# Attention and ternary FFN on one core: SP's DMA queue put into the program's order from the second unit on

## The chip, the core and the metric

One core of one Trainium2 chip runs the whole kernel in one launch. The metric is the device time of one execution in microseconds (us). The kernel before takes 1697.4 us (median of three executions, 1696.96 to 1698.08).

Engines go by the profile's names: PE (matmuls; PEld are its weight loads), DVE (vector), ACT (scalar), POOL (GpSimd) and SP. SP computes nothing here: it issues all DMAs, one after the other. When the next DMA in its program has to wait for data, everything behind that DMA waits too.

## The reference

x is 8 x 1024 x 256 in fp32. With LN a layernorm without weights:

```python
x = x + LN(attention(LN(x)) @ Wo)
x = x + LN(ffn(LN(x)))
# attention: q = h @ Wq (16 heads of 16), k, v = h @ Wk, h @ Wv (4 heads, each shared by 4 query heads);
#   rotary embedding on q and k; softmax(q k^T / sqrt(256)) v, no mask
# ffn: (h @ ternary(W).T) * alpha + bias, ternary(W) in {-1, 0, 1} by a threshold on mean |W|
```

## The kernel before

The 8192 rows are cut into 16 **units** of 512 queries; two units make one batch. A unit is worked through as four numbers i (i = 4u + j, j from 0 to 3; one head of each group for all 512 queries), each i in 8 **steps** (one tile of 128 keys), each step in four **quarter steps**. So a unit has 128 quarter steps. In one quarter step PE makes one matmul of scores for the exponentials (se, L676), one matmul of scores for the row maxima of a later i (sm, L603), and some matmuls of values (av, L712). ACT takes the exponentials (e, L692), DVE the maxima (mx, L628).

The softmax shift of an i goes into the score product itself: its maxima are joined (mc, L645), transposed on PE (pm, L651), copied by ACT (mh, L653), split by DVE (ml, L660) and written by two 8-KB DMAs (q_st<-ml, L667, function `shift_low`) into rows of the stacked queries q_st. The first se matmul of that i reads those rows, so it waits for the first of the two DMAs.

Beside this main loop run two chains that are cut into parts. Each part is put at a step of a unit by a table:

- **Project** (table P_PARTS) makes queries, keys and values of a unit three units ahead: layernorm, transposes (pt_xt), products (pkv, pq), rotary embedding on POOL. Keys go through DRAM twice: d_k<-kv_t (L434) and back as k_rot (L438, in `kv_and_dram`), then dk<-ks (L451, in `kt`, four DMAs) and back into the stacked keys k_st (L502, `stack_keys`, six DMAs). Queries go out as dq<-hlq (L493, `q_to_dram`, four DMAs). A unit ahead of their use they come back as q_st (L567, `stack_queries`: six DMAs of 256 KB and two fills, L146). I call these eight DMAs the **stack**.
- **Tail** (table T_PARTS) finishes the unit before. The sums av go to DRAM, one store for each i (d_av<-avsb, L733). `fetch` loads them as xn (L763, two DMAs) and their denominators as den (L768). `invert` takes the reciprocal on DVE, stores it (d_rec<-den, L775) and loads it spread over the rows (a<-d_rec, L780, two DMAs). `scale` multiplies xn by a on POOL (L786) and splits the result into a high and a low part, hl (L157, L162). `attn` multiplies hl by Wo on PE (pa, L302). Then follow layernorms, residual sums, the FFN (pt_ot, pf) and the store out_x<-a (L856, in `end`). A product pa reads hl of both halves c of the features. It makes the products of the high parts first and those of the low parts last.

What orders the work: the function `window` writes out the main loop, two to four quarter steps at a time, and puts due parts behind them. Inside `manual_schedule` the named engines keep the order in which the code issues; all others are ordered by a list scheduler at build time. For PE, DVE and ACT the order is written by hand in the whole loop. SP and POOL are ordered by the scheduler. Each DMA uses one of eight semaphores in turn, so it waits until the DMA eight places before it has landed.

Of the kernel before, what the change touches and what calls it, by code (L numbers as in the profile page):

```python
# [8 lines left out]
F32 = mybir.dt.float32  # L9
# [7 lines left out]
P = 128  # L17
# [3 lines left out]
HD = 16  # L21
UT = 4
UQ = UT * P
# [5 lines left out]
def kernel(  # L29
# [29 lines left out]
    nc = tc.nc  # L59
    B, S, D = x.shape  # L60
    DK = HKV * HD
# [7 lines left out]
    SPU = G * NK  # L69
# [5 lines left out]
    small = ctx.enter_context(tc.tile_pool(name="small", bufs=4))  # L75
    work = ctx.enter_context(tc.tile_pool(name="work", bufs=2))
    qkp = ctx.enter_context(tc.tile_pool(name="qkp", bufs=1))
# [29 lines left out]
    for src, lo, n in ((w_q, 0, D), (w_k, D, DK), (w_v, ROT, DK)):  # L107
        nc.sync.dma_start(
            out=wqkv[:, :, lo : lo + n], in_=src.rearrange("(c p) n -> p c n", p=P)
# [18 lines left out]
    nc.sync.dma_start(out=bias_bc, in_=bias.partition_broadcast(P))  # L128
    alpha_bc = const.tile([P, 1], F32, name="alpha_bc")
    nc.sync.dma_start(out=alpha_bc, in_=alpha.partition_broadcast(P))  # L130


    k_st, v_aug, q_st = [], [], []
# [30 lines left out]
    def split(eng, hi, lo, src, hi_eng=None):  # L164

        split_hi(hi_eng or eng, hi, src)
        split_lo(eng, lo, src, hi)
# [25 lines left out]
    ffn = {}  # L193
# [119 lines left out]
    def rotate(eng, x, cos, sin, t2):  # L313

        for dst, table in ((t2, sin), (x, cos)):
            eng.tensor_tensor(dst, x, table.unsqueeze(1).to_broadcast(list(x.shape)), ALU.mult)  # L316
        eng.tensor_tensor(x[:, 0], x[:, 0], t2[:, 1], ALU.subtract)
        eng.tensor_tensor(x[:, 1], x[:, 1], t2[:, 0], ALU.add)
# [5 lines left out]
    class Project:  # L324
# [103 lines left out]
        def kv_and_dram(self):  # L428

            u = self.u  # L430
            for p in range(2):
                self.kv(p)
            d_k = dram.tile([DK, UQ], F32, tag="d_k", name=f"d_k_{u}")
            nc.sync.dma_start(out=d_k, in_=self.kv_t[:DK])  # L434
            self.k_rot = qkp.tile([P, 2, P], F32, tag="k_rot", name=f"k_rot_{u}")
            src = d_k.rearrange("(m e) (g t) -> e g m t", e=2, t=P)
            for e in range(2):
                nc.sync.dma_start(out=self.k_rot[:, e, :], in_=src[e])  # L438

        def kt(self):  # L440
            rotate(
                self.eng, self.k_rot, cos_kt_sb[:, self.half], sin_kt_sb[:, self.half],
                work.tile([P, 2, P], F32, tag="t2k", name=f"t2k_{self.u}", bufs=1),
            )
            hl = qkp.tile([P, 2, 2, P], F32R, tag="k_parts", name=f"ks_{self.u}")
            split(self.eng, hl[:, 0], hl[:, 1], self.k_rot)
            dk = self.dk = dram.tile([2, DK, UQ], F32, tag="dk", name=f"dk_{self.u}")
            dst = dk.rearrange("l (m e) (g t) -> l e g m t", e=2, t=P)
            for l in range(2):
                for e in range(2):  # L450
                    nc.sync.dma_start(out=dst[l, e], in_=hl[:, l, e, :].bitcast(F32))  # L451
            self.stack_keys()

        def q_product(self, p):
            if self.q_rot is None:
# [31 lines left out]
        def q_to_dram(self):  # L487
            dq[self.u] = dram.tile([2, D, UQ], F32, tag="dq", name=f"dq_{self.u}")
            rows = dq[self.u].rearrange("l (b c i e) t -> l c b i (e t)", c=2, e=2, i=HD // 2)
            for l in range(2):  # L490
                for c in range(2):
                    src = self.hl["q"][64 * c : 64 * (c + 1), l].rearrange("p e t -> p (e t)")
                    nc.sync.dma_start(out=rows[l, c], in_=src.bitcast(F32))  # L493
# [176 lines left out]
    es, av_ps, av_sb, d_av = {}, {}, {}, {}  # L670
# [65 lines left out]
    class Tail:  # L736
# [21 lines left out]

        def fetch(self):

            for c in range(2):
                self.on[c] = self.new("xn", c)
                nc.sync.dma_start(  # L763
                    out=self.on[c].rearrange("p t d -> p (t d)"),
                    in_=d_av[self.u][8 * c : 8 * c + 8, 0:HD, :],
                )
            self.den = small.tile([P, UQ // 8], F32, tag="den", name=f"den_{self.u}", bufs=1)
            nc.sync.dma_start(  # L768
                out=self.den, in_=d_av[self.u][:, HD, :].rearrange("i (g t) -> i g t", g=8)
            )  # L770

        def invert(self):
            nc.vector.reciprocal(self.den, self.den)
            d_rec = dram.tile([2, 2 * HKV, UQ], F32, tag="d_rec", name=f"d_rec_{self.u}")
            nc.sync.dma_start(  # L775
                out=d_rec.rearrange("c i (g t) -> (c i g) t", g=8), in_=self.den
            )
            for c in range(2):
                self.a[c] = self.new("a", c)
                nc.sync.dma_start(  # L780
                    out=self.a[c].rearrange("p t d -> p (t d)"),
                    in_=d_rec[c].unsqueeze(1).to_broadcast([2 * HKV, HD, UQ]),
                )
# [66 lines left out]
        def end(self, p):  # L850
            u, f = self.u, self.a[p]
            ln_apply(self.eng(p), f, f, self.sc[p])
            self.eng(p).tensor_tensor(f, self.x1[p], f, ALU.add)
            b, half = divmod(u, UPB)
            tiles = out[b, half * UQ : (half + 1) * UQ, :].rearrange("(t p) d -> p t d", p=P)
            nc.sync.dma_start(out=tiles[:, self.tiles(p), :], in_=f)  # L856

    class LastTail(Tail):

# [76 lines left out]
    def at(step, f, *args):  # L936
        assert step >= -START
        todo.setdefault(step, []).append((f, args))
# [22 lines left out]
    def load(u):  # L961
# [3 lines left out]

    P_PARTS = (
        (26, "begin", 0), (33, "xw", 0), (37, "begin", 1), (43, "xw", 1), (49, "kv_and_dram"), (51, "q", 0), (52, "kt"), (53, "v"), (55, "q", 1),
        (57, "q_to_dram"),
    )
    L_PARTS = (  # L970
        (10, "n", 0), (13, "o", 0), (15, "attn", 0), (16, "stats_a", 0), (19, "stats_x", 0),
# [2 lines left out]
        (29, "attn", 2), (29, "x", 1), (30, "stats_a", 2), (30, "ffn", 1), (31, "stats_f", 1),  # L974
    )
    T_PARTS = (
        (1, "fetch"), (7, "invert"), (8, "scale", 0), (9, "scale", 1), (12, "attn", 0),
        (15, "attn", 1), (15, "stats_a", 0), (17, "stats_a", 1), (19, "stats_x", 0),
        (22, "xw", 0), (23, "stats_x", 1), (26, "ffn", 0), (27, "xw", 1), (31, "ffn", 1),
        (31, "stats_f", 0), (33, "stats_f", 1),  # L980
    )

    P_FIRST = (47, 51, 54, 57, 59, 60, 62, 61, 63, 64)
    T_LAST = (1, 3, 4, 5, 9, 10, 11, 14, 17, 19, 20, 22, 25, 27, 24, 28)

    warm = []

# [60 lines left out]
        for k, (_, *p) in zip(steps, P_PARTS):  # L1048
            at(start + k, part, projects, u, *p)
    for u in range(2, NU):  # L1050
        at(SPU * (u - 1) + 1, stack_queries, u)
    for u in range(NU - 1):
        start = SPU * (u + 1)
        at(start + 1, begin_tail, u)
        steps = [k for k, *_ in T_PARTS] if u < NU - 2 else T_LAST
        for k, (_, *p) in zip(steps, T_PARTS):
# [5 lines left out]
    def maxima_by(s):  # L1062

        return s + 4 * START + 2 * sum(s >= k for k in (28, 36, 52, 68, 84, 100))
# [13 lines left out]
    def window_size(s):  # L1078


        left = 4 * NK - s % (4 * NK)
        if s >= ends:
            return 4
        if s == 6:
            return 2
        size = min(2 if s >= REGULAR and any(banked(*p) for p in ready) else 3, left, ends - s)
        if left - size == 1:
            size += 1 if size == 2 else -1
        return size
# [23 lines left out]
    def take_low():  # L1113
        while split_later:
            shift_low(split_later.pop(0))
# [12 lines left out]
    def av_windows(lag):  # L1128

        while len(behind) > lag:  # L1130
            i, s, size = behind.pop(0)
            first = s % (4 * NK)
            av_piece(i, first * P, (first + size) * P)
            if first + size == 4 * NK:
                done.append(i)

    def window(s):


        late, size = s >= ends, window_size(s)  # L1140
        if done:
            av_out(done.pop())
        if late:
            for r2 in range(2):
                exp_two(s // 4, r2)
        else:
            end = min(maxima_by(s + size), 4 * NSTEP)
            for q in range(max(size, end - maxima[0])):
                if q < size:
                    exp_one(s + q)  # L1150
                if maxima[0] < end:
                    max_scores(maxima[0])
                    maxima[0] += 1
                if q == 0:
                    take_low()
            reduce_early(maxima[0])
        take_low()
        behind.append((s // (4 * NK), s, size))
        for n in range(s // 4, (s + size) // 4):
            collect(n)  # L1160
        do_parts(3 - size if REGULAR <= s < ends else 99)
        av_windows(1 if late else 2)
        return s + size

    E = mybir.EngineType
    due, picks = [], []
    with tc.manual_schedule(engines={E.PE, E.DVE, E.Activation, E.Pool}):
# [52 lines left out]
        s = 0  # L1220
        while s < 8:
            s = window(s)
    with tc.manual_schedule(engines={E.PE, E.DVE, E.Activation}):
        while s < 4 * NSTEP:
            s = window(s)
        av_windows(0)
        av_out(NU * G - 1)
        assert not (todo or due or ready or split_later)
# [70 lines left out]
```

## Time and profile before

| | |
|---|---|
| time, median of three executions | 1697.4 us |
| the profiled execution: its own time, its span | 1696.64 us, 1694.9 us |
| mean granted TensorE clock | 0.972 |
| busy: PE, DVE, ACT, POOL | 94%, 83%, 74%, 49% |
| DMA queue of SP | 115.60 MB, its packets 29.4% of 16 engines' span |
| chain that ended last | PE 59%, DVE 22%, DMA 9% |

How to read it. A unit takes 98.7 to 102.5 us in units 2 to 12 (from its first se matmul to the next unit's), so a stall of 1 us that comes once in each unit costs about 1% of the time. A row "X <- Y: total, times, longest" says how long X stood idle until Y ended. Rows of the timeline begin with the start in us from the beginning of the span, then the length; for SP the length is only the issuing, not the transfer. The granted clock is 1.00 or 0.50 at any moment; a mean between them says how much of the stretch ran at half speed.

### The profile page before, as it was taken

The numbers are of one execution on the slowest core, as the hardware profiler recorded it, in microseconds if no ns is written. First come the engines' busy times: TensorE is split into PE (matmuls) and PEld (weight loads), VectorE is DVE, ScalarE is ACT, GpSimd is POOL, SyncE is SP. The second block draws the span as 40 slices with busy tenths as digits, with TensorE's granted clock in tenths as the row PEclk, the third lists the DMA queues.
The fourth block names the chain that finished last, engine by engine and source line by source line (L and its number), as shares of the span: only waits on it lengthen the run. The fifth ranks groups of instructions, "written<-read, shape, count | busy, mean of one in ns | idle before, by whom it ended". The sixth has DMA issues, their size and how long they took to land.

```text
span 1694.9 us, 36717 instructions
## 1 busy us (share of the span) xinstructions
PE 1598.8 (94%) x14440; PEld 811.3 (48%) x14440; DVE 1398.7 (83%) x2054; ACT 1246.4 (74%) x2423; POOL 838.5 (49%) x1239
## 2 busy tenths in 40 slices
PE   7989899999999999999999999999999999999997
PEld 5544454444545444444444445444444544444444
DVE  7778788979798797978889798797978879998864
ACT  4657677778687786877778687686867768787875
POOL 5541456374554646455464645536455453333444
PEclk8999999999999999999999999999999999999999
DMA  4151514125151432515133151412415124141100
GB/s 134 51 98 37 122 43 95 54 73 98 48 98 57 81 72 65 113 42 100 49 86 80 54 115 45 94 55 71 88 46 100 36 76 74 33 85 33 41 14 26
DMA packets 86077, 117.95 MB, mean 70 GB/s; under 512 B 12088, under 2 KB 50808, under 8 KB 85752
## 3 DMA queue, kind: packets, MB, share of 16 engines
q1 hardware_dynamic: 85904, 115.60, 29.4%
q8 instruction: 114, 1.87, 0.5%
q14 instruction: 59, 0.48, 0.1%
HBM read 68.65 MB, written 45.88 MB: 68 GB/s over the span
## 4 chain that ended last, share of the span: by engine, by line
PE 59%; DVE 22%; DMA 9%; POOL 3%; issue 3%; SPq 2%; ACT 2%; POOLq 0%; ACTq 0%; DVEq 0%
PE av L712 21%; PE se L676 19%; DVE mx L628 18%; PE sm L603 8%; PE pa L302 3%; DMA q_st<-ml 2%; PE pq L302 2%; PE pf L302 2%; DMA dk<-ks 2%; DMA k_rot<-d_k 2%; PE pkv L302 1%; DVE bnst L237 1%; PE pt_ot L279 1%; DMA d_k<-kv_t 1%; ACT e L692 1%
## 5 line engine op out<-in xcount | busy, mean ns | idle before, releaser
L628 DVE TENSOR_REDUCE mx<-sm 128x2 f32<-128x1024 f32 (+1 forms) x1309 | 1205.2, 970 | 244.5 <-PE sm L603 191.3
L692 ACT ACTIVATE e<-se 128x512 f32<-128x512 f32 x1996 | 1053.2, 603 | 301.4 <-PE sm L603 256.6
L603 PE MATMUL sm<-k_st,q_st 64*128 64x512 f32 x2048 | 756.6, 453 | 16.6 <-DVE mx L628 7.7
L676 PE MATMUL se<-q_st,k_st 64*128 64x512 f32 x2048 | 721.7, 448 | 48.4 <-DMA q_st<-ml 42.7
L712 PE MATMUL av<-e,v_aug 128*32 128x256 f32 (+2 forms) x8560 | 612.1, 383 | 0.0
L676 PEld LDWEIGHTS se<-q_st,k_st 64*128 64x128 f32 x2048 | 330.0, 187 | 418.6 <-ACT e L692 240.2
L603 PEld LDWEIGHTS sm<-k_st,q_st 64*128 64x128 f32 x2048 | 329.1, 188 | 94.5 <-DVE mx L628 73.3
L712 PEld LDWEIGHTS av<-e,v_aug 128*32 128x32 f32 x8560 | 196.7, 109 | 233.6 <-issue 171.6
L241 POOL TENSOR_SCALAR lnsc<-mv 128x2 f32<-128x2 f32 (+1 forms) x134 | 25.8, 193 | 287.2 <-DVE mv L239 280.8
L786 POOL TENSOR_TENSOR xn<-xn,a 128x512 f32<-128x512 f32 x30 | 38.5, 1284 | 156.3 <-DMA a<-d_rec 153.9
L242 POOL TENSOR_TENSOR lnsc<-lnsc,mhalf 128x2 f32<-128x2 f32 (+1 forms) x134 | 92.5, 691 | 0.9
L846 POOL TENSOR_TENSOR a<-a,bias_bc 128x512 f32<-128x512 f32 x30 | 38.6, 1285 | 97.9 <-ACT a L845 97.9
L253 POOL TENSOR_SCALAR xn<-x,lnsc 128x256 f32<-128x256 f32 x116 | 65.1, 569 | 2.2
L157 POOL TENSOR_SCALAR ot<-ot 128x512 fp32r<-128x512 f32 x30 | 18.6, 621 | 83.9 <-ACT ot L283 63.7
L316 POOL TENSOR_TENSOR t<-q_rot,sin_q_sb 128x512 f32<-128x512 f32 x31 | 39.8, 1285 | 39.9 <-ACT q_rot L460 39.9
L157 POOL TENSOR_SCALAR xt<-xt 128x512 fp32r<-128x512 f32 x26 | 16.2, 622 | 65.3 <-ACT xt L283 65.3
L302 PE MATMUL pq<-xt,wqkvh 128*128 128x256 f32 x256 | 47.9, 313 | 0.4 <-ACT e L692 0.4
L302 PE MATMUL pa<-woh,hl 128*128 128x256 f32 x240 | 46.2, 294 | 1.1 <-ACT e L692 1.1
L237 DVE BATCH_NORM_STATS2 bnst<-x 128x6 f32<-128x256 f32 x124 | 45.9, 412 | 0.6 <-DMA x<-in_L_attn_x 0.6
L237 DVE BATCH_NORM_STATS2 bnst<-a 128x6 f32<-128x256 f32 x120 | 44.5, 413 | 0.0
L302 PEld LDWEIGHTS pq<-xt,wqkvh 128*128 128x128 f32 x256 | 38.3, 208 | 13.0 <-issue 11.6
L162 POOL TENSOR_TENSOR hlq<-q_rot,hlq 128x512 fp32r<-128x512 f32 x31 | 39.5, 1275 | 7.0 <-ACT hlq L159 4.5
(165 smaller groups left out, 1298.0 us busy)
## 6 DMA issues: line engine op xcount, KB each, us to landing
q_st<-dq SPq DMA_DIRECT2D x90, 256.0 KB
dq<-hlq SPq DMA_DIRECT2D x60, 256.0 KB
d_av<-avsb SPq DMA_DIRECT2D x60, 256.0 KB
x<-in_L_attn_x SPq DMA_DIRECT2D x15, 512.0 KB
xn<-d_av SPq DMA_DIRECT2D x30, 256.0 KB
a<-d_rec SPq DMA_DIRECT2D x30, 256.0 KB
xr<-in_L_attn_x SPq DMA_DIRECT2D x15, 512.0 KB
out_x<-a SPq DMA_DIRECT2D x30, 256.0 KB
```

Source lines behind the costliest of these rows:

```text
L162: eng.tensor_tensor(lo, src, hi.bitcast(F32), ALU.subtract)
L237: nc.vector.bn_stats(st[:, t, :], src[:, t, :])
L242: nc.gpsimd.tensor_tensor(sc[:, 1, :], sc[:, 1, :], mhalf[:, :n], ALU.pow)
L253: eng.tensor_scalar(dst[:, t, :], src[:, t, :], sc[:, 0, t : t + 1] if eng is nc.gpsimd else mv[:, t, 0:1], sc[:, 1, t : t + 1], ALU.add i ...
L302: nc.tensor.matmul(out, chunk(left[i], c), chunk(right[j], c), start=(k == 0), stop=(k == len(steps) - 1),)
L316: eng.tensor_tensor(dst, x, table.unsqueeze(1).to_broadcast(list(x.shape)), ALU.mult)
L603: scores = nc.tensor.matmul(sm[0][:, part, :], queries[rows], k_st[(u // UPB) % 3][rows, r2, ch * 512 : (ch + 1) * 512], start=True, stop= ...
L628: early[0] = nc.vector.tensor_reduce(mx[i][:, a, head_and_tile(i, r2, t), lo:n], sm[0][:, lo:n, :], AX.X, ALU.max).ins
L676: nc.tensor.matmul(sc if len(queries.shape) == 2 else sc.rearrange("p (j t) -> p j t", j=G), k_st[(i // G // UPB) % 3][rows, r2, kt * P : ...
L692: nc.scalar.activation(e, sc, AF.Exp, scale=1.0 / D**0.5)
L712: nc.tensor.matmul(av_ps[0][32 * r : 32 * r + 32, lo:hi], va[:, kt, r, :], es[i * NK + kt, r // 2, r % 2][:, lo:hi], start=(kt == 0 and lo ...
L846: eng.tensor_tensor(f, f, bias, ALU.add)
```

## The change

From quarter step 128 on (the second unit), SP too is ordered by hand. Transfers whose data come late are put into a list by `later(n, f)` and issued n windows further down. `fetch` loads the denominators ahead of the sums. `stack_queries` moves from step 1 to step 6 of its unit, `q_to_dram` from 57 to 62, and the early parts of the tail by one to three steps; DVE's and PE's parts move along with them. POOL stays with the scheduler.

```diff
+    def later(windows, f):
+        if running[0]:
+            postponed.append((window_number[0] + windows, f))
+        else:
+            f()
+    def queue_postponed(all_of_them=False):
+        for entry in list(postponed):
+            if all_of_them or entry[0] <= window_number[0]:
+                postponed.remove(entry)
+                entry[1]()
...
 # kv_and_dram
-            nc.sync.dma_start(out=d_k, in_=self.kv_t[:DK])
...
+            later(1, lambda: nc.sync.dma_start(out=d_k, in_=self.kv_t[:DK]))
+            later(3, fetch)          # fetch(): the two loads of k_rot
...
 # kt
+            later(4, store)          # store(): the four stores dk<-ks
+            later(7, self.stack_keys)
...
 # Tail.fetch: den<-d_av now ahead of the two xn<-d_av
 # Tail.invert
+            later(1, ...)            # d_rec<-den
+            later(3, lambda: self.load_factors(d_rec))   # the two loads a<-d_rec
 # Tail.end
-            nc.sync.dma_start(out=tiles[:, self.tiles(p), :], in_=f)
+            later(3, lambda: nc.sync.dma_start(out=tiles[:, self.tiles(p), :], in_=f))
...
-        (57, "q_to_dram"),
+        (62, "q_to_dram"),
...
     T_PARTS = (
-        (1, "fetch"), (7, "invert"), (8, "scale", 0), (9, "scale", 1), (12, "attn", 0),
-        (15, "attn", 1), (15, "stats_a", 0), (17, "stats_a", 1), (19, "stats_x", 0),
-        (22, "xw", 0), (23, "stats_x", 1), (26, "ffn", 0), (27, "xw", 1), (31, "ffn", 1),
+        (1, "fetch"), (7, "invert"), (10, "scale", 0), (11, "scale", 1), (14, "attn", 0),
+        (16, "attn", 1), (16, "stats_a", 0), (18, "stats_a", 1), (20, "stats_x", 0),
+        (23, "xw", 0), (24, "stats_x", 1), (27, "ffn", 0), (28, "xw", 1), (31, "ffn", 1),
...
-    T_LAST = (1, 3, 4, 5, 9, 10, 11, 14, 17, 19, 20, 22, 25, 27, 24, 28)
+    T_LAST = (1, 5, 8, 9, 11, 12, 13, 15, 17, 19, 20, 22, 25, 27, 24, 28)
...
-        at(SPU * (u - 1) + 1, stack_queries, u)
+        at(SPU * (u - 1) + 6, stack_queries, u)
...
 # window
+        window_number[0] += 1
+        running[0] = s >= 4 * SPU
...
+        queue_postponed()            # behind the window's se and sm, ahead of its parts
...
     with tc.manual_schedule(engines={E.PE, E.DVE, E.Activation}):
+        while s < 4 * SPU:
+            s = window(s)
+    with tc.manual_schedule(engines={E.PE, E.DVE, E.Activation, E.SP}):
         while s < 4 * NSTEP:
             s = window(s)
+        running[0] = False
+        queue_postponed(True)
```

In the built programs the middle of a unit on SP reads, before: dk x4, k_st x6, q_st<-ml (j = 3), xn_0, d_av, dq x4, q_st<-ml (j = 0), the stack, d_av, out_x, xn_1, den, out_x, q_st<-ml (j = 1), d_rec, a x2, d_av, q_st<-ml (j = 2), d_av, d_k, k_rot x2. After: d_av, out_x, xr, den, xn x2, out_x, q_st<-ml (j = 1), the stack, d_rec, d_av, a x2, q_st<-ml (j = 2), d_av, d_k, k_rot x2, x, q_st<-ml (j = 3), dk x4, d_av, k_st x6, q_st<-ml (j = 0), dq x4. (Here the j given is that of the i whose shift is written.)

More of the change, by code (lines that the diff above doesn't have):

```diff
@@ L130 @@
     nc.sync.dma_start(out=alpha_bc, in_=alpha.partition_broadcast(P))
+    postponed, window_number, running = [], [0], [False]
+    def later(windows, f):
[8 more added lines that the diff above has]
+                entry[1]()
     k_st, v_aug, q_st = [], [], []
@@ L433, in kv_and_dram, with fetch @@
             d_k = dram.tile([DK, UQ], F32, tag="d_k", name=f"d_k_{u}")
-            nc.sync.dma_start(out=d_k, in_=self.kv_t[:DK])
[L435 to L438, printed above, removed]
+            def fetch():
+                self.k_rot = qkp.tile([P, 2, P], F32, tag="k_rot", name=f"k_rot_{u}")
+                src = d_k.rearrange("(m e) (g t) -> e g m t", e=2, t=P)
+                for e in range(2):
+                    nc.sync.dma_start(out=self.k_rot[:, e, :], in_=src[e])
+            later(1, lambda: nc.sync.dma_start(out=d_k, in_=self.kv_t[:DK]))
+            later(3, fetch)
         def kt(self):
@@ L448, in kt, with store @@
             dst = dk.rearrange("l (m e) (g t) -> l e g m t", e=2, t=P)
[L449 to L452, printed above, removed]
+            def store():
+                for l in range(2):
+                    for e in range(2):
+                        nc.sync.dma_start(out=dst[l, e], in_=hl[:, l, e, :].bitcast(F32))
+            later(4, store)
+            later(7, self.stack_keys)
         def q_product(self, p):
@@ L489, in q_to_dram, with store_q @@
             rows = dq[self.u].rearrange("l (b c i e) t -> l c b i (e t)", c=2, e=2, i=HD // 2)
+            self.store_q(rows)
+        def store_q(self, rows):
             for l in range(2):
@@ L759, in fetch @@
         def fetch(self):
+            self.den = small.tile([P, UQ // 8], F32, tag="den", name=f"den_{self.u}", bufs=1)
+            nc.sync.dma_start(
+                out=self.den, in_=d_av[self.u][:, HD, :].rearrange("i (g t) -> i g t", g=8)
+            )
             for c in range(2):
@@ L766, in fetch @@
                 )
[L767 to L770, printed above, removed]
         def invert(self):
@@ L774, in invert, with load_factors @@
             d_rec = dram.tile([2, 2 * HKV, UQ], F32, tag="d_rec", name=f"d_rec_{self.u}")
-            nc.sync.dma_start(
+            later(1, lambda: nc.sync.dma_start(
                 out=d_rec.rearrange("c i (g t) -> (c i g) t", g=8), in_=self.den
-            )
+            ))
+            later(3, lambda: self.load_factors(d_rec))
+        def load_factors(self, d_rec):
             for c in range(2):
```

## Prediction

> **What bounds the kernel now.** I read the page's busy shares first, then PE's waits, SP's timeline, and busy time by stretch around the longest wait.
>
> ```profile
> PE 1598.8 (94%) x14440; PEld 811.3 (48%) x14440; DVE 1398.7 (83%) x2054; ACT 1246.4 (74%) x2423; POOL 838.5 (49%) x1239
> ```
>
> PE sets the pace; what can be gained is its idle and slow time. PE's waits have one large row:
>
> ```profile
> PE se L676 <- DMA q_st<-ml: 42.7, 16, 5.7
> ```
>
> The first score matmul of an i waits for its shift row. From the second unit on there are 13 such stalls: 5.77 us in unit 1 (i = 5), then one each in units 2 to 12 at j = 3, 1.98 to 3.28 us; 36.9 us in all (starts of successive se matmuls). Unit 5 is my example: i = 20 to 23, start T0 = 587.03. SP's timeline shows the cause there:
>
> ```profile
> 651.05 2.37 SPq L451 DMA_DIRECT2D dk<-ks  x4
> 654.68 2.98 SPq L502 DMA_DIRECT2D k_st<-dk  x6
> 657.76 1.43 SPq L667 DMA_DIRECT2D q_st<-ml  x2
> ```
>
> DVE had ml ready at 652.23. It stood 5.5 us behind ten key transfers; PE went on at 659.88. The stall costs more than itself (columns: stretch, length, busy PE, PEld, DVE, ACT, POOL, granted clock, DMA):
>
> ```profile
> 658.00:662.00 4.00, 2.12 (x24) 1.25 (x24) 1.34 (x2) 1.56 (x3) 1.86 (x3) 0.94 0.11 30
> 662.00:666.00 4.00, 4.00 (x28) 2.81 (x24) 2.10 (x5) 1.29 (x3) 1.89 (x2) 0.63 0.26 72
> 666.00:670.00 4.00, 4.00 (x38) 1.73 (x32) 2.72 (x4) 3.77 (x8) 3.38 (x5) 1.00 0.17 66
> ```
>
> After the stall the clock is halved for 3.41 us (6.83 us after longer ones). The eight quarter steps behind it take 8.39 us here and 6.91 us in unit 7, whose 2.15-us stall was not followed by half clock. These extras (0 to 2.86 us) add up to 25.2 us over the 13 stalls. Check: unit 7 without its stall is 98.67 - 2.15 = 96.5 us; unit 5 is 100.72 - 2.71 - 1.48 = 96.5; twelve units sum to 1220.2, and 1220.2 - 12 x 96.5 = 62.
>
> **Term 1, the stall that goes: -62 us.** In the built order after, q_st<-ml for j = 3 stands ahead of dk and k_st, behind only k_rot and a load of x whose data are there long before. Issued when ready (652.2) it lands 2.0 to 2.7 us later, as undisturbed ones do. PE could use it at 657.2 (659.88 - 2.7). A layernorm statistic now stands before ml on DVE (two 0.41 and two 0.17 us = 1.2 us); against that pq_1 (2.3 us of PE) now stands before the matmul that waits. What is late next there: nothing within 2 us. Bounds: -62 and 0.
>
> **Term 2, the load that comes late instead.** The stack is moved into the middle of the chain den, d_rec, a, hl, pa. Before, it ran ahead of all that:
>
> ```profile
> 583.77 1.26 SPq L567 DMA_DIRECT2D q_st<-dq  x3
> 586.76 0.29 SPq L146 DMA_DIRECT2D q_st<-fill_d  x1
> 591.12 0.34 SPq L733 DMA_DIRECT2D d_av<-avsb  x1
> 600.98 0.66 SPq L763 DMA_DIRECT2D xn<-d_av  x1
> ...
> 609.83 0.35 SPq L775 DMA_DIRECT2D d_rec<-den  x1
> 611.85 1.48 SPq L780 DMA_DIRECT2D a<-d_rec  x2
> ```
>
> Issuing the stack takes 3.3 us, but by the semaphores its last DMA lands 15.7 us after its first issue (14.9 to 17.0 in units 2 to 14, mean 15.9). And what is issued behind it lands behind it: d_av, issued at 591.12, landed at 600.96, 0.2 us after the stack, where an undisturbed one takes 2.0. SP's waits in that stretch say the same:
>
> ```profile
> SPq L763 <- DMA d_av<-avsb: 8.3, 1, 8.3
> ```
>
> After, the store d_rec stands directly behind the stack, and both loads a wait for it. POOL and PE then follow as here:
>
> ```profile
> 615.74 1.28 POOL L786 TENSOR_TENSOR xn<-xn,a 128x512 f32<-128x512 f32 x1 [8.05 <-DMA a<-d_rec]
> 617.39 1.29 POOL L786 TENSOR_TENSOR xn<-xn,a 128x512 f32<-128x512 f32 x1 [0.37 <-DMA a<-d_rec]
> 618.65 1.21 POOL L157 TENSOR_SCALAR hl<-xn 128x512 fp32r<-128x512 f32 x2
> 619.82 2.53 POOL L162 TENSOR_TENSOR hl<-xn,hl 128x512 fp32r<-128x512 f32 x2
> ```
>
> ```profile
> 624.24 0.50 PE L302 MATMUL pa<-woh,hl 128*128 128x256 f32 x2
> ```
>
> hl is complete at T0 + 35.3 and pa starts at T0 + 37.2: 1.9 us of slack. Now the times after, from T0:
> - ml (j = 1) is ready at 15.3 before. After, two more quarter steps and the FFN product pf (8 matmuls, 1.2 us) stand before its transpose, and a statistic (1.2 us) before it on DVE: about 19.2. Its two issues take 1.45, so the stack starts at 20.7 and has landed at 20.7 + 15.9 = 36.6; d_rec at 36.8.
> - Before, d_rec landed at 24.8. So a, and with it hl, come 12.0 us later (POOL's order of these six operations is unchanged).
> - pa stands six quarter steps further down (3.3 us in the list of se starts), plus 1.2 for pf: 4.5 us later.
> - PE waits 12.0 - 1.9 - 4.5 = 5.6 us, less some 0.3 because the first matmuls of pa need only the high parts: **5.3 us**, in units 1 to 14, which all have a stack and a tail: **+74 us**. With the stack at 14.9 and 17.0, the issue of ml 1 us either way, and up to 0.8 us of pa done early, it is 3.5 to 6.7: 49 to 94.
>
> Nothing covers this wait: pa is on PE, in order. DVE and ACT are not behind there (2.53 and 2.65 us busy of 4 at 622 to 626), so nothing is made up later. On SP, d_av and ml for j = 2 stand behind the waiting loads. ml is due at T0 + 45.8 before and would be issued near 38, so it is in time.
>
> **Term 3, half clock after the new stalls.** No row shows it at this place; bounds 0 (unit 7) and 2.86 (the longest extra). I take the mean of the 13 old stalls, 25.2/12 = 2.1 us a unit: **+29 us** (0 to 40). Here the Trainium skill differs: "TensorE: Matmul & The Clock Gate", section on HAM oscillation, sees the danger in PE gaps above some 3.4 us; pa's wait comes in two pieces, each shorter. In this trace gaps of 2.0 to 3.3 us were followed by half clock 11 times in 12. By the page alone the term would be nothing.
>
> **Term 4, POOL's new order.** In the build after, xn for pt_ot (first half) stands behind the second half's residual work, all behind the load k_rot: 13.8 us of POOL work plus gaps after k_rot instead of 10.0. k_rot is there 7.4 us after pkv's last matmul; so xn is ready at 21.6. PE gets from there to pt_ot in 17.3 us before (without the stall) and in 20.3 after (one quarter step and pq_1 more). PE waits 0 to 3 us; I take 1.2 in 12 units: **+14 us** (0 to 36).
>
> **At nothing** (cover, and price without it): denominators first (two 0.65-us issues change places; DVE's reciprocal waits for its place at T0 + 22.2 anyhow; if late, up to the 3.6 us that den takes to land); out_x, dq, dk, k_st, each unit (used a unit or more later, or only stored; a buffer that came late would cost the 5.5 us seen in SP's queue); T_LAST (no stack in the last unit; pa moves two steps, about the 6 us that the later reciprocal takes; between -3 and +3 us).
>
> **Sum,** against the profiled execution (1696.64 us, span 1694.9; 0.8 below the median 1697.4): 1696.6 - 62 + 74 + 29 + 14 = **1751 us**. With the terms' own ends: 1696.6 - 62 + 49 + 15 + 0 = 1699, and 1696.6 - 62 + 94 + 40 + 30 = 1799.
>
> **Rivals.**
> - *The stack doesn't hold d_rec back* (faster). The store is small; were it to land in 2.0 us beside the stack, hl would be on time and terms 2 and 3 gone: 1696.6 - 62 + 14 = 1649. It decides from the point where the stack lands 5.3 us earlier, in 10.6 us instead of 15.9. For it: the stack's packets leave the DMA engines idle most of the time (its stretch has a DMA share of 1.1 in 4 us). Against it: d_av and out_x behind every stack. The Trainium skill speaks for it: "DMA: Bandwidth & Descriptors", section "Queues, rings and completion order", says that completion isn't first-in-first-out per issuing engine. The 9.8 us of d_av here show otherwise for these shapes. By the page's sentence the time would be 1649.
> - *The stall of j = 3 stays as well* (slower): if k_rot or x hold the queue up as dk and k_st did, term 1 falls away: 1813.
> - *Break-even*: the wait at pa and its clock come to about 3.4 us a unit, as term 1 less term 4 gives: within 3 us of 1697.
>
> **Chances.** Forecast 0.68 (own range 1699 to 1799); not held back, 0.15; stall stays, 0.11; break-even, 0.06. A difference of 0.2% (3.4 us) is about what a measurement of this kernel can tell from none. Faster 0.17 (0.15 and part of break-even), same 0.03, slower 0.80. The range reaches from break-even to the second rival, 1690 to 1815, and leaves out 0.15.
>
> **What would show it.** Right: no row q_st<-ml above a few us in PE's waits; a new row of PE or PEld waiting for POOL hl at pa, some 5 us a unit, half clock behind it; d_rec landing 15 us after the stack's first issue; POOL's wait for a<-d_rec longer. Wrong: pa without a wait, or a wait for q_st<-ml left at j = 3. The weakest step is the instant at which PE reaches pa: it is a difference of two chains of some 25 us each.

## The result, and the profile after

The kernel after took **1759.05 us** (median of 4 runs, 1754.41 to 1761.59), the kernel before 1697.18 us beside it (4 runs, 1693.96 to 1698.08): a ratio of 1.0365, 95% interval 1.0339 to 1.0391. It is slower, by 8 us more than forecast. The profiled execution of after took 1758.97 us (span 1757.2).

T0 is the start of a unit's first score matmul; times in the fences run from the beginning of the span. The lengths of the units (T0 to the next T0) say where the 62.3 us of span came from:

| part of the run | before, us | after, us | difference |
|---|---|---|---|
| units 0 and 1 | 285.2 | 287.7 | +2.5 |
| units 2 to 12 | 1112.4 | 1159.4 | +47.0 |
| units 13 and 14 | 182.0 | 187.3 | +5.3 |
| unit 15 to the end | 115.2 | 122.8 | +7.6 |

The first row says little of the change: 2.0 of its 2.5 us fall in unit 0, which the change does not touch and which takes 112.5 to 117.9 us in the thirteen profiled kernels of this case.

PE's waits, after (us in all, times, longest):

```profile
PE pa L318 <- POOL hl L173: 32.6, 21, 3.5
PE se L703 <- DMA q_st<-ml: 22.9, 5, 8.6
PE sm L630 <- DVE mx L655: 19.1, 61, 1.0
PE pa L318 <- POOL hl L178: 14.8, 26, 0.8
PE se L703 <- ACT e L719: 13.5, 30, 0.5
```

The row q_st<-ml fell from 16 waits to 5, and two rows at pa are new, as forecast. The third and the fifth were smaller before, and the forecast had nothing for them:

```profile
PE sm L603 <- DVE mx L628: 7.7, 25, 1.0
PE se L676 <- ACT e L692: 3.2, 7, 0.5
```

Two of the five waits left for ml are long: one of 7.5 us in unit 1, and one of 8.6 us in the last unit, which is new.

SP in unit 5 (T0 = 604.9; columns: start, length, instruction):

```profile
623.69 1.41 SPq L694 DMA_DIRECT2D q_st<-ml  x2
625.15 2.76 SPq L594 DMA_DIRECT2D q_st<-dq  x6
627.96 0.58 SPq L162 DMA_DIRECT2D q_st<-fill_d  x2
629.51 0.35 SPq L802 DMA_DIRECT2D d_rec<-den  x1
632.10 0.35 SPq L760 DMA_DIRECT2D d_av<-avsb  x1
642.59 1.34 SPq L810 DMA_DIRECT2D a<-d_rec  x2
```

d_rec is issued at 629.51 and the loads that wait for it go out at 642.59: 13.1 us for a store of 32 KB. In units 2 to 12 the mean is 12.3 us (2.3 before). POOL's row of the wait for a doubled (before 153.9 us):

```profile
L816 POOL TENSOR_TENSOR xn<-xn,a 128x512 f32<-128x512 f32 x30 | 38.1, 1271 | 318.1 <-DMA a<-d_rec 314.2
```

Then PE at pa in the same unit, and the clock behind it (in the second fence: stretch, length, busy PE, PEld, DVE, ACT, POOL, granted clock, DMA share, GB/s):

```profile
646.07 0.39 PE L630 MATMUL sm<-k_st,q_st 64*128 64x512 f32 x1
649.60 0.39 PE L318 MATMUL pa<-woh,hl 128*128 128x256 f32 x1 [3.13 <-POOL hl L173]
...
652.65 1.01 PE L318 MATMUL pa<-woh,hl 128*128 128x256 f32 x3 [0.64 <-POOL hl L178]
```

```profile
647.00:655.00 8.00, 4.33 (x20) 3.09 (x24) 0.91 (x1) 0.76 (x2) 7.22 (x8) 0.69 0.02 5
655.00:659.00 4.00, 4.00 (x38) 1.75 (x34) 1.65 (x2) 1.96 (x5) 0.00 (x0) 0.76 0.00 0
```

PE is idle 3.13 us and then 0.64 us (with two pieces of some 0.2 us 4.2 us in all), and from 650.1 on the clock is halved for 6.83 us, through pa and the scores behind it. Ten of the units 2 to 12 show 6.83 us, one 3.41 us.

### The profile page after: what moved, and what is told of

It reads as the page before. It is cut to its first block, busy times and chain, and to the rows that moved or that the text cites. A ratio compares the mean times of both kernels' runs of the same rounds, so it can differ in the third digit from the quotient of the medians.

```text
span 1757.2 us, 36136 instructions
## 1 busy us (share of the span) xinstructions
PE 1622.9 (92%) x14240; PEld 818.3 (47%) x14240; DVE 1393.7 (79%) x2028; ACT 1247.8 (71%) x2423; POOL 831.7 (47%) x1239
## 4 chain that ended last, share of the span: by engine, by line
PE 60%; DVE 19%; DMA 10%; POOL 6%; ACT 2%; issue 2%; SPq 1%; POOLq 0%; DVEq 0%; ACTq 0%
PE av L739 21%; PE se L703 20%; DVE mx L655 14%; PE sm L630 7%; DMA d_rec<-den 5%; PE pa L318 3%; PE pq L318 3%; POOL hl L178 2%; PE pf L318 2%; DMA a<-d_rec 2%; DMA q_st<-ml 2%; DVE bnst L253 2%; ACT e L719 1%; PE pkv L318 1%; DMA q_st<-dq 1%
## 5 line engine op out<-in xcount | busy, mean ns | idle before, releaser
L739 PEld LDWEIGHTS av<-e,v_aug 128*32 128x32 f32 x8360 | 190.5, 110 | 235.9 <-issue 179.2
L318 PE MATMUL pa<-woh,hl 128*128 128x256 f32 x240 | 65.2, 361 | 48.1 <-POOL hl L173 32.6
L843 ACT COPY a<-pa 128x512 f32<-128x512 f32 x30 | 17.6, 585 | 95.1 <-POOL xt L178 76.1
L318 PEld LDWEIGHTS pa<-woh,hl 128*128 128x128 f32 x240 | 44.2, 228 | 69.1 <-POOL hl L173 41.0
L332 POOL TENSOR_TENSOR t2k<-k_rot,sin_kt_sb 128x256 f32<-128x256 f32 x14 | 10.3, 733 | 79.0 <-DMA k_rot<-d_k 79.0
```

The costliest lines, as they stand in the source:

```text
L318: nc.tensor.matmul(out, chunk(left[i], c), chunk(right[j], c), start=(k == 0), stop=(k == len(steps) - 1),)
L739: nc.tensor.matmul(av_ps[0][32 * r : 32 * r + 32, lo:hi], va[:, kt, r, :], es[i * NK + kt, r // 2, r % 2][:, lo:hi], start=(kt == 0 and lo ...
```

## Experiments

Eleven kernels were run. "Before" in a ratio is the kernel before, run beside each on the same chip.

**1. The stack in two halves** (theory: the stack ahead of d_rec makes pa late)

```
-        at(SPU * (u - 1) + 6, stack_queries, u)
+        at(SPU * (u - 1) + 6, stack_queries, u, (0,))     # a = 0: 3 loads, 1 fill
+        at(SPU * (u - 1) + 12, stack_queries, u, (1,))    # a = 1
```

> The kernel after with one edit: q_st's stack goes out in two halves, one l of the split at step 6 and the other at step 12, so that 4 of its 8 DMAs instead of 8 stand ahead of the store d_rec. Theory (the whole stack ahead of d_rec makes pa late, and PE's gaps there bring the half clock): half a stack lands in about half of 16 us, so d_rec lands some 8 us earlier, hl is there before PE reaches pa, and both the gaps (3.8 us a unit by the trace of the kernel after) and the half clock behind them are gone in units 2 to 12: about 11 x 7.5 us less, 1759 - 82 = 1677 us (1665 to 1690), with no row of PE waiting for POOL hl at pa above 5 us in sum. Rival A (pa waits for POOL's own new order, not for the stack): no change, 1759 within 5. Rival B (the second half, now behind the loads a, comes too late for the unit's first scores): a new wait for q_st, 1759 or more.

(The halves are those of a, three loads and one fill each, not those of l, as the expectation has it.)

Measured: 1679.3 us (1678.02 to 1680.16), ratio 0.9904 [0.9878, 0.9931]. d_rec lands 5.8 us behind its issue in units 2 to 12, at T0 + 29.7 instead of 37.2. No row of pa is left among PE's larger waits, and units 2 to 12 show one record of half clock (3.41 us). The third and the fifth row above stay nearly as they were:

```profile
PE sm L630 <- DVE mx L655: 18.4, 59, 1.0
PE se L703 <- ACT e L719: 13.5, 30, 0.5
```

Terms 2 and 3 together are worth 78.9 us of span (1757.2 - 1678.3). The forecast had 103. The seven units of 2 to 12 without a stall take 98.2 us here, not the 96.5 of before: 1.8 us a unit is something else. The other four (5 to 8) take 99.6 to 100.6 us: there pt_ot waits 0.9 to 1.5 us for POOL's xn, the wait of Term 4.

**2. pa two steps later** (theory: only the meeting of hl and PE counts)

```
-        ... (14, "attn", 0), (16, "attn", 1), (16, "stats_a", 0), (18, "stats_a", 1), (20, "stats_x", 0),
+        ... (16, "attn", 0), (18, "attn", 1), (18, "stats_a", 0), (19, "stats_a", 1), (21, "stats_x", 0),
```

> The kernel after with one edit: the steps attn 14 and 16 go to 16 and 18 (stats_a to 18 and 19, stats_x of half 0 to 21), so that pa stands two steps further down on PE, and the stack stays where it is. Theory (it is only a meeting of hl and PE: PE comes to pa some 3 to 4 us before hl is there): pa's gaps and the half clock behind them are gone, about 11 x 7 us: 1759 - 77 = 1682 us (1670 to 1700). Rival A (the load on SP's queue itself costs the time, wherever pa stands): 1759 within 5. Rival B (what follows pa, the FFN half and the projection's operands on POOL and DVE, has no slack for two steps): the pa row goes, and another row of PE, behind x1's transposes or pf, takes its place: 1720 to 1759.

Measured: 1742.6 us (1742.03 to 1744.2), ratio 1.028 [1.0248, 1.0312]: rival B. pa no longer waits, and the clock stays full there. In its place stands

```profile
PE pt_ot L295 <- POOL xn L269: 61.2, 12, 5.2
```

some 5.1 us a unit, with 6.83 us of half clock behind it. The later tail puts its layernorm work on POOL in between the projection's, so xn comes later: from the start of POOL's work on k_rot until xn is complete it takes 19.9 us in unit 5, against 13.6 in after and 10.0 before. This is the wait that Term 4 feared. pa can't be moved out of the way by itself.

**3. The keys behind ml, alone** (Term 1, in the kernel before)

```
-            for l in range(2): ...  nc.sync.dma_start(out=dst[l, e], ...)   # dk, in kt
-            self.stack_keys()
+        def keys_out(self):                       # a part of its own, at step 55
+            with tc.issue_after(shifts[max(shifts)]):
+                ...                               # the four dk
+                self.stack_keys()
```

> The kernel before with one part of the change alone: the four stores dk and the loads k_st go out behind the ml transfer of j = 3 instead of ahead of it; all else, the stack's place too, is as before. Theory (term 1: the j = 3 stall of units 2 to 12 with its half clock is caused by these transfers ahead of ml, and costs what a unit with it, 101.1 us, has over one without, 96.5): 11 x 4.6 = 51 us less, 1697 - 51 = 1646 us (1635 to 1655); no row of PE waiting for q_st<-ml at j = 3. Rival A (k_rot and xr, still ahead of ml, hold it up as well): 1697 within 10. Rival B (the half clock comes at this point of a unit from DVE's load, not from the stall): only the idle time of the stall itself goes, some 2.8 us a unit: 1666.

Measured: **1643.1 us** (1638.98 to 1644.88), ratio 0.9688 [0.966, 0.9715]. Units 2 to 12 take 1061.3 us in all, 51.1 less than before, and show no half clock. PE's largest row is

```profile
PE se L682 <- DMA q_st<-ml: 13.4, 4, 6.1
```

of which 6.1 us is the one stall of unit 1. Rival B (half clock from DVE's load) falls. Nothing of the rest of the change was needed for this gain.

**4. The last unit's xr behind ml**

```
-            self.xr = load_x(u, "xr", 1)
+            later(12 if u == NU - 1 else 0, self.load)     # load(): the same load_x
```

> The kernel after with one edit: in the last unit the tail's load of xr, which waits on SP for GpSimd to be done with the tile x, goes out 12 windows later, behind the ml transfers of i = 62 and 63. Theory (the last unit's loss against the kernel before is PE's stall for ml of i = 62, issued 12.9 us after it was ready because this load stood ahead of it in program order): the stall of 8.5 us goes, 1759 - 7.6 = 1751 us (1748 to 1753). Rival (the last unit is longer because of the tail's new order, T_LAST): 1759 within 2.

Measured: 1752.9 us (1743.54 to 1762.37, 6 runs), ratio 1.0345 [1.0311, 1.038]. That interval overlaps after's, so the time alone decides nothing; the traces do. In after, SP stood at the load of xr until POOL was done with x:

```profile
SPq L91 <- POOL x L848: 30.1, 1, 30.1
```

```profile
1654.61 1.36 SPq L810 DMA_DIRECT2D a<-d_rec  x2
1686.20 0.37 SPq L91 DMA_DIRECT2D xr<-in_L_attn_x  x1
1686.67 1.38 SPq L694 DMA_DIRECT2D q_st<-ml  x2
```

ml of i = 62 was ready at 1673.81 and went out 12.9 us later. With the edit it goes out 0.06 us after it is ready, PE's stall of 8.5 us is gone, and the last unit takes 117.3 us instead of 122.8. Of its 7.6 us, 5.5 are this wait. The other 2.1 are left; a wait of 2.3 us at pt_ot for POOL's xn, which before does not have, stands in this unit of the experiment and is about as long, but no run tests it.

**5. Work in place of the wait** (how much of the loss is the clock?)

```
             pa = psum([P, self.width, D], f"pa_{self.u}_{p}")
+            for _ in range(9 if p == 0 and 2 <= self.u <= 12 else 0):
+                nc.tensor.matmul(pa[:, 0, :], wo_s[0][:, 0, :P], wo_s[0][:, 0, :], start=True, stop=True)
```

> The kernel after with one edit: ahead of pa's first real product in units 2 to 12, PE runs 9 matmuls of 128x256 whose result is overwritten (start=True follows), so that it works through most of the wait for hl; they add work and take none away. Theory (each gap of about 3 us at pa is followed by 6.8 us of half clock, which costs about as much again as the gap): the gap shrinks below 1 us, the half clock behind it goes, and 11 x 3.4 us are saved less up to 1 us a unit where the junk is longer than the wait: 1759 - 37 = 1722 us (1717 to 1735). Rival (the half clock there comes from something else than the gap, such as the mix of work in this stretch): no half clock saved, 1759 to 1770.

Measured: 1751.5 us (1749.4 to 1755.65), ratio 1.0339 [1.0318, 1.036]. Neither number came: 8 us less, not 37. The edit counts by the unit whose tail it is, and pa of a unit's tail runs one unit later: the nine matmuls stand in units 3 to 13, and unit 2 (105.5 us, 6.83 us of half clock) has none. In units 3 to 12 they didn't always cover the wait. What was left of the first gap ranged from under 0.5 to 2.2 us, and the half clock went with it only in part. That makes a series of its own, by units 3 to 12:

| half clock in the unit | units | mean length, us |
|---|---|---|
| 6.83 us | 3, 4, 8, 9, 10, 12 | 105.6 |
| 3.41 us | 5, 7, 11 | 103.9 |
| none | 6 | 102.5 |

So units with 6.83 us of half clock are 3.1 us longer than the one with none. As PE is also idle 0.7 us longer in them, the half clock alone cost 2.5 to 3.1 us a unit. That the clock goes with the gaps is shown by experiments 1 and 2, where pa doesn't wait and the clock stays full there, more than by this one: 0.95, 0.62 and 0.72 us in unit 3 were followed by 6.83 us, 0.62 and 0.84 us in unit 5 by 3.41, and 0.56, 0.62 and 0.84 us in unit 6 by none.

**6. The stack behind ml (j = 1), alone** (Term 2, in the kernel before)

```
-        at(SPU * (u - 1) + 1, stack_queries, u)
+        at(SPU * (u - 1) + 6, behind_shift, 4 * (u - 1) + 1, stack_queries, u)
```

> The kernel before with one part of the change alone: the stack goes out directly behind the ml transfer of j = 1, ahead of d_rec; every other order is as before (the four dk and six k_st transfers still ahead of ml of j = 3, pa at its old step). Theory (term 2 alone, with its old meeting point): the stack, issued from T0 + 17, lands at about T0 + 33, d_rec behind it and x at about 34 instead of 24.7, hl 9 to 10 us later, and PE, which has 1.9 us of slack there, waits some 7.5 us a unit at pa in units 1 to 14, with 3 us of half clock behind it in units 2 to 12: 1697 + 14 x 7.5 + 11 x 3 = 1835 us (1790 to 1870). Rival A (the place of the stack alone does nothing without the fixed order of SP): 1697 within 10. Rival B (the two stalls share one loss, because a unit that stalls at pa no longer stalls at j = 3): 1750 to 1790.

Measured: 1830.1 us (1822.37 to 1831.96), ratio 1.0784 [1.0753, 1.0816]. The price of the new place is 137 us where pa stands at its old step; d_rec lands 11.5 us behind its issue.

```profile
PE pa L302 <- POOL hl L157: 78.0, 16, 6.9
PE se L676 <- DMA q_st<-ml: 37.8, 14, 4.1
```

Both stalls stand in one unit (5.0 us at pa and 2.2 us at j = 3 in unit 5), each with its half clock; they don't share one loss. The same place of the stack costs 79 us in after, where pa stands later.

**7. The stack on ScalarE's queue** (what holds d_rec?)

```
-                nc.sync.dma_start(out=q_st[u % 2][row : row + HD].bitcast(F32), ...
+                (nc.scalar if u > 1 else nc.sync).dma_start(out=q_st[u % 2][row : row + HD].bitcast(F32), ...
```

> The kernel after with one edit: the stack's 8 DMAs of units 2 to 15 are issued by ScalarE instead of SP, at the same place of the program's order; d_rec stays on SP. Theory (order within SP's queue holds d_rec back, not the work of the DMA engines): d_rec lands within 3 us of its issue instead of 13, pa's gaps and their half clock go (1759 - 82 = 1677), and ScalarE pays for the issues, 3.3 us a unit by SP's time for the same eight, of which PE may see all: 1677 to 1735 us. Rival A (the engines that move the stack are what d_rec waits for): d_rec still lands 10 us or more behind its issue, pa's rows stay, 1759 or more. Rival B (part of both): d_rec lands 5 to 8 us behind its issue.

Measured: 1743.5 us (1739.16 to 1745.78), ratio 1.0286 [1.0264, 1.0307]. The time lies between the cases; d_rec decides. SP in unit 5 (T0 = 599.2):

```profile
618.01 1.42 SPq L696 DMA_DIRECT2D q_st<-ml  x2
623.02 0.34 SPq L804 DMA_DIRECT2D d_rec<-den  x1
629.34 0.34 SPq L762 DMA_DIRECT2D d_av<-avsb  x1
636.41 1.37 SPq L812 DMA_DIRECT2D a<-d_rec  x2
```

SP's queue holds nothing of the stack now, and d_rec still takes 13.4 us (mean of units 2 to 12: 13.0): it lands at 636.3, 0.2 us behind the last DMA of the stack. Rival A is right on this: **not the order in a queue holds d_rec back, but the DMA engines' work.** The stack went through a queue of its own (packets, MB, share of 16 engines):

```profile
q1 hardware_dynamic: 73696, 92.66, 18.0%
q10 hardware_dynamic: 12208, 22.94, 10.2%
```

and while it ran the engines were full:

```profile
621.00:625.00 4.00, 1.32 (x12) 0.34 (x10) 1.99 (x3) 0.63 (x2) 0.00 (x0) 1.00 1.10 150
629.00:633.00 4.00, 4.00 (x38) 1.91 (x38) 3.86 (x7) 3.76 (x8) 0.00 (x0) 1.00 1.12 132
```

The DMA column is the mean share of the 16 engines: at 1.1 the packets of each engine add up to more than the whole stretch. pa's wait shrank for another reason: PE now loses time earlier, at 621 to 625, because ScalarE stands still for 3.4 us at the eight DMAs and the scores' e come late (63.4 us in PE's row of waits for e, 15.6 of it in unit 1 alone). Not all of the 3.4 us is issuing: the last of the eight goes out only when the first has landed, which is a wait of 1.2 us.

**8. The dq stores of unit 3 later.** Base: experiment 3.

```
-    P_FIRST = (47, 51, 54, 57, 59, 60, 62, 61, 63, 64, 63)
+    P_FIRST = (47, 51, 54, 57, 59, 60, 62, 61, 63, 76, 63)
```

> The kernel of the run with the dk and k_st transfers alone behind ml (1643 us), with one edit: the first late unit's dq stores go 12 steps later, behind the ml transfers of i = 5 and i = 6. Theory (the one long stall left there, 6.0 us at i = 5, comes from ml of i = 5 issued 8.9 us late, because den waits for d_av, which lands behind these stores): the stall goes, 1643 - 6 = 1637 us (1633 to 1640). Rival (den and xn hold ml back also without the stores): 1643 within 2.

Measured: 1645.8 us (1643.65 to 1647.35), ratio 0.9711 [0.9694, 0.9728], no gain. It tells nothing of the cause: the scheduler, which orders SP in this kernel, still issued the stores ahead of ml of i = 5. But the trace showed a better suspect: d_av of unit 1, issued 1.4 us after the last DMA of a stack, took 12.2 us, and the loads behind it, which wait for it, held ml.

**9. The stack back at step 1.** Base: the kernel after.

```
-        at(SPU * (u - 1) + 6, stack_queries, u)
+        at(SPU * (u - 1) + 1, stack_queries, u)
```

> The kernel after with one edit: the stack goes out at step 1 as in the kernel before, so that it has landed before d_rec is stored; all the rest of the change stays. Theory (with the stack out of d_rec's way nothing is left of terms 2 and 3; what stays is some 1.8 us a unit of waits behind DVE and ACT): like the split stack or a little faster, 1677 us (1668 to 1684), no row of PE waiting for POOL hl, no half clock in units 2 to 12. Rival (the fixed order of SP needs the stack out of the unit's first transfers: at step 1 it holds up den and xn instead): units of 100 us or more, above 1695.

Measured: 1804.4 us (1802.82 to 1808.94), ratio 1.0641 [1.0616, 1.0665]. My theory was wrong and the rival right: units of 107 to 109 us, with

```profile
PE se L703 <- DMA q_st<-ml: 132.9, 18, 15.9
```

SP in unit 5 (T0 = 617.1) shows why:

```profile
625.37 2.81 SPq L594 DMA_DIRECT2D q_st<-dq  x6
...
631.70 0.60 SPq L789 DMA_DIRECT2D den<-d_av  x1
633.62 2.58 SPq L794 DMA_DIRECT2D xn<-d_av  x2
637.63 0.40 SPq L886 DMA_DIRECT2D out_x<-a  x1
639.61 1.94 SPq L694 DMA_DIRECT2D q_st<-ml  x2
```

The scheduler of the kernel before issued this stack at T0 - 3.3, behind the ml of j = 0. In program order it goes out at T0 + 8.2. ml of j = 1, ready at 635.92, goes out 3.7 us late and lands 11.2 us after it was ready, behind the stack's work and the loads of xn: a 7.4-us gap of PE, and 10.24 us of half clock. So with SP in program order both places hurt: step 1 delays ml, step 6 delays d_rec.

**10. The tail's parts back at their old steps.** Base: experiment 9.

```
-        ... (14, "attn", 0), (16, "attn", 1), (16, "stats_a", 0), (18, "stats_a", 1), (20, "stats_x", 0),
-        (23, "xw", 0), (24, "stats_x", 1), (27, "ffn", 0), (28, "xw", 1), ...
+        ... (12, "attn", 0), (15, "attn", 1), (15, "stats_a", 0), (17, "stats_a", 1), (19, "stats_x", 0),
+        (22, "xw", 0), (23, "stats_x", 1), (26, "ffn", 0), (27, "xw", 1), ...
```

> The kernel of the run with the stack at step 1, with one edit more: the tail's parts from attn to ffn at the steps that they had in the kernel before (scale stays at 10 and 11). Theory (the 1.8 us a unit that a split stack leaves over the unit with the keys alone, 98.2 against 96.4, come from the tail's later steps, which put a layernorm statistic and two products into the first quarter of the next unit, where DVE's mx is due): units of 96.5 us and 'PE sm <- DVE mx' down from 18 to about 8 us: 18 us less than the run with the stack at step 1, about 1659 us. Rival (they come from SP's fixed order, the late stores and loads): no change from the run with the stack at step 1.

Measured: 1762.9 us (1759.56 to 1765.59), ratio 1.0391 [1.0367, 1.0414]: 41 us below experiment 9, more than the 18 expected. ml's row fell too (to 112.9 us), so the time is no clean price. The two rows are:

```profile
PE sm L630 <- DVE mx L655: 6.6, 22, 1.0
...
PE se L703 <- ACT e L719: 2.7, 6, 0.5
```

From 19.2 and 13.5 us to 6.6 and 2.7: these waits come from the tail's new steps, not from SP's order. What counts is where a part stands, not that it stands later: in experiment 2, where five of these nine parts stand later still, the rows are down too, to 8.6 and 8.1 us.

**11. Unit 1 put in order as well.** Base: experiment 3.

```
+            if u == 3 and p == ["q_to_dram"]:
+                at(start + 77, behind_shift, 6, part, projects, u, *p)
...
+        if u == 2:
+            at(SPU + 12, behind_shift, 6, stack_queries, u)
```

> The kernel of the run with the dk and k_st transfers alone behind ml (1643 us), with one edit: in unit 1 the stack of unit 2 and the dq stores of unit 3 go out behind the ml transfer of i = 6. Theory (the stall of 6 to 8 us at i = 5 comes from the stack of 12 us of DMA work ahead of d_av, on which SP waits with ml of i = 5 behind it): d_av lands in about 2 us, ml of i = 5 goes out when it is ready, unit 1 shrinks from 104.3 to about 97: 1643 - 7 = 1636 us (1632 to 1640). Rival (the stall moves to the next transfer, d_rec or the loads a in unit 1): 1640 to 1650.

Measured: **1638.4 us** (1637.65 to 1644.58), ratio 0.9669 [0.9645, 0.9692], the fastest version. Unit 1 takes 101.4 us instead of 104.3, and ml's row is down to

```profile
PE se L682 <- DMA q_st<-ml: 5.5, 3, 2.7
```

The interval overlaps that of experiment 3, so only the trace shows the gain in unit 1. The 97 us expected there were not reached: at T0 + 72.7 pt_ot waits 1.9 us for POOL's xn, and 6.83 us of half clock stand there.

## Why the prediction was right

The direction and the mechanism of Terms 1 to 3 were right. The total was near because errors met, and that is luck. For units 2 to 12, in which the change does nearly all its work:

| step | forecast | measured, units 2 to 12 | by |
|---|---|---|---|
| Term 1, the stall at j = 3 goes | -62 (13 stalls) | -51 | experiment 3 |
| Term 2, PE waits at pa | +74 (14 units) | +44 (4.0 a unit) | PE's idle time, after less experiment 1 |
| Term 3, half clock behind it | +29 | +35 (3.2 a unit) | the rest of after less experiment 1 |
| Term 4, pt_ot waits for POOL | +14 | 0 | trace of after |
| at nothing | 0 | +20 (1.8 a unit) | experiments 1 and 3 |

The measured column gives +48; the lengths gave +47.0. That they agree proves nothing: the column goes from before over experiments 3 and 1 to after, by the same lengths. (Terms 2 and 3 together: units of 105.4 us in after, 98.2 in the undisturbed ones of experiment 1, 11 x 7.2 = 79. PE is idle 6.8 us of a unit in after and 2.75 in those of experiment 1: 4.0 of the 7.2. The other 3.2 are time in which PE works, but slower; experiment 5 has 2.5 to 3.1 for that. The 1.8 is 98.2 - 96.4.)

**Term 1** was right for units 2 to 12: 4.65 us a unit against 62/13 = 4.8. It was wrong in unit 1. I counted the stall at i = 5 among those that go, though no key transfer stands ahead of ml there. It stayed, at 7.5 us of PE's time, but for another reason than before. In before and in experiment 3 it came from a stack ahead of d_av, as experiment 11 shows. In after that stack goes out behind this ml; here ml, ready at 194.08, went out at 200.41, behind four stores dq, d_av, two loads xr and the loads den and xn, and landed 7.5 us after that. No run tests which of these held it.

**Term 2** had the chain right: the stack's start at 20.7 (20.3 in unit 5), d_rec's landing at 36.8 (37.2 on average), pa's place at 41.7 (41.6). The step that failed is its last, "less some 0.3 because the first matmuls of pa need only the high parts". pa began 3.0 us before hl was complete (T0 + 44.7 and 47.7 in unit 5), and PE used that time for part of pa: its gaps come to 4.2 us there, not 5.3. And units 1, 13 and 14, counted at the full price, have small gaps or none.

**Term 3** was too small a unit (2.1 against 2.5 to 3.2): I took the mean over 13 stalls of which seven were followed by 6.83 us of half clock, five by 3.41 and one by none, and here it is 6.83 in ten units of eleven. Nor does the stall's length alone decide, as "6.83 us after longer ones" says: before, 2.0 us in unit 3 brought 6.83, and 2.6 to 2.7 in units 4 to 6 brought 3.41. That +29 comes as near to +35 as it does is only because it counts 14 units instead of 11. The Trainium skill's "TensorE: Matmul & The Clock Gate", section "HAM oscillation — how this bites in real kernels", gives the rule of gaps above some 3.4 us. By it this term would be nearly nothing: of the ten units with 6.83 us, two have a gap of 3.5 us, and in the other eight the longest gap is 1.9 to 3.4 us.

**Term 4** was 0 here, but only just: in unit 5 xn was complete at T0 + 81.8, and pt_ot began at 81.9. PE came there late because it had waited at pa. Where that wait was gone, pt_ot waited for xn: 5.0 us in all in experiment 1, 61.2 us in experiment 2.

**What I had at nothing** cost 20 us in the middle and 7.6 us at the end. The first was in plain sight: I found the statistic that now stands before ml on DVE and the FFN product in the first quarter, and charged them to the instants of ml and pa alone, not to the score loop that shares DVE and ACT with them. PE's added waits are 1.0 of the 1.8 us a unit (2.75 us idle against 1.78 in experiment 3); where the other 0.8 us come from no run shows. For the second I looked at T_LAST and at pa alone, not at what SP must pass in program order in the last unit: one load that waits 30.1 us (experiment 4: 5.5 of the 7.6).

**Slips in the working** that changed little: the stalls at j = 3 stand in units 1 to 12, not 2 to 12 (with i = 5 they make the 13); the stack in unit 5 landed 17.0 us after its first issue, not 15.7 (the sum goes by the mean, 15.9); Term 4's 7.4 and 13.8 us make 21.2, not 21.6; and the two totals with the terms' own ends take 15 for Term 3's lower end, which is 0, and 30 for Term 4's upper end, which is 36. With these the range is 1684 to 1805.

**The rival "the stack doesn't hold d_rec back"** could have been closed before the run. I read the DMA share of 1.1 in a 4-us stretch as 1.1 us of 4, and concluded that the engines were mostly idle. The column is a share, not a time. The DMA slices of before around this stack (40 slices from 583 to 606, 9 means 90% or more) and of after (from 623 to 645):

```profile
DMA  0009999999999999999999999999311002469540
```

```profile
DMA  0000029999999999999999999999997701100035
```

25 slices of 0.575 us and 24 of 0.55 us: the engines are full for 13 to 14 us on end, in before too. The Trainium skill bears on it in "DMA: Bandwidth & Descriptors". Its section "Issuing engines are not separate DMA queues" has all DMAs run on the same 16 engines, whoever issues them, and experiment 7 agrees: 13.0 us on a queue apart, 12.3 us on the same one. The sentence that I weighed, in "Queues, rings and completion order", says that completion is not first-in-first-out per issuing engine. The same passage says that the engines take descriptors in ring order, and that a completion lands only behind all earlier writes of its DMA engine, across queues. I quoted the one half and not the other.

What stays open: why d_rec on a queue apart passes none of the stack's work; why gaps of 0.6 to 0.95 us were sometimes followed by half clock and sometimes not; which transfer held ml in unit 1 of after; what the other 2.1 us of the last unit are.

## What to carry to other kernels

A transfer that was harmless early becomes a delay where you move it: ask which small transfer of a chain to PE is issued within its landing time, and look at the share of the DMA engines, not at the queue. An order fixed for a whole queue takes every wait with it, so fix only the pair that hurts: one part of this change, ordering ten key transfers behind ml, gave 3.1% by itself, and all of it together cost 3.7%. When a step of a list is moved, charge its work to every loop that shares its engine, not only to the chain that you follow.

## What the runs showed of the hardware

- Six loads of 256 KB into 16 partitions each, with two fills, kept all 16 DMA engines full for about 13 us at some 100 to 150 GB/s (after, unit 5); in units 1 to 14 of after the last landed 15 to 19 us after the first issue. A 32-KB store issued within that time took 12.3 us on the same queue and 13.0 us on another; behind half of these loads 5.8 us, and 2.3 us where they had landed before.
- Half clock followed gaps of PE much shorter than itself, 6.83 us behind pieces of 0.95, 0.62 and 0.72 us (experiment 5), and such records cost 2.5 to 3.2 us each (experiment 5; after less experiment 1).
- Eight DMAs issued by ScalarE kept it from its own work for 3.4 us, of which 1.2 us was a wait of the last one until the first had landed (experiment 7, unit 5).
